# A sparse graph transformer on one core: turned x kept in weight places, five key stores, another GpSimd order

## The chip, the cores and the metric

The kernel runs on one core of one Trainium2 chip. The metric is the device time of one execution in microseconds (us), as the median of several runs; lower is better. The engines are named as in the profile: PE multiplies matrices, DVE is VectorE, ACT is ScalarE, POOL is GpSimd, SP is SyncE, which here only issues transfers.

## The reference

Two layers of a graph transformer on 2708 tokens of width 512, with 8 heads of 64 and a feed-forward width of 2048, all in float32. A token attends to its neighbours only: `adj` is a symmetric 2708 x 2708 int32 matrix with ones on the diagonal, in which an entry elsewhere is 1 with a chance of about 0.3%. So a token has some nine entries in its list, and 24 places are enough for the longest list.

```python
def layer(h, adj, ...):                       # twice, with weights of its own
    mask = adj.astype(jnp.float32) + jnp.eye(n)
    q = (h @ Wq.T + bq).reshape(n, 8, 64)     # k and v in the same way
    scores = jnp.einsum('nhd,mhd->hnm', q, k) / 8.0
    scores = jnp.where(mask[None] == 0, -1e9, scores)
    attn = jax.nn.softmax(scores, axis=-1)
    ctx = jnp.einsum('hnm,mhd->nhd', attn, v).reshape(n, 512)
    h1 = layer_norm(h + ctx @ Wo.T + bo, ln1_g, ln1_b)
    ff = relu(h1 @ W1.T + b1) @ W2.T + b2
    return layer_norm(h1 + ff, ln2_g, ln2_b)
```

## The kernel before, in words

**Tiles.** The tokens are cut into 22 tiles (`NT`) of up to 128; the last has 20 tokens. The kernel never forms the full score matrix. For each token it makes a list of neighbours, gathers their key and value rows from DRAM by indirect DMA, and multiplies on DVE and ACT. PE does the dense projections and the feed-forward.

**The first stage, `first`.** It works through the tiles in the order 20, 21, 0 to 19. For each it projects K and V on PE (L576) from blocks of the transposed input (`xg`, 256 tokens each, 11 blocks, 0.5 MB for a full one), adds the bias on the way into a tile `kvs` (K on DVE at L914, V on ACT), and stores `kvs` to the DRAM table `kv_d` through ACT's queue. Beside this run the lists (`lists`): SP loads 128 rows of the adjacency matrix (`aj`, 1.354 MB, two buffers), POOL adds the diagonal (L689), ACT squares it into codes (L693), and DVE finds the neighbours with MAX8 (L696). W1 and W2, the feed-forward weights, come in eight pairs of pieces, in places of their own in the pool `wts`: `w1_0` to `w1_7` and `w2_0` to `w2_7`, of 0.5 MB each. Until the weights arrive, some of these places hold other things. Before the change three of them (`w1_5` to `w1_7`) take the x blocks in rotation, three (`w2_5` to `w2_7`) the `kvs` tiles, and four (`w1_3`, `w1_4`, `w2_3`, `w2_4`) the tables of the lists.

**The second stage, `first_queries`.** It projects Q for every tile (tile 18 first, then 19, 20, 21, and 0 to 17; the counter is `j`, 0 to 21). As the three places of x have been turned over by then, nearly all x blocks are loaded a second time, by the same function `load`. DVE scales the result into `qs` (L977), which SP stores. Meanwhile the tokens are sorted by the length of their lists, so that tiles of similar tokens need few slots. DVE works out each token's new place (`ranks`, L803), POOL moves the lists of 21 tiles to their new places in the DRAM table `rec_d` by indirect DMA (L809), reads the table back as `new` (L823 and L831), and casts the token numbers to integers (`ident_i`, L842); from `new` DVE makes the row numbers `idx` and the mask `minus` (L845, L846, function `listed`). The first part of `listed` covers tiles 17, 18 and 19, the second the others.

**Attention ahead.** While PE projects Q, the function `advance` lets the generator `attend` run ahead. Tile 20 of the sorted order is made of the tokens of tile 18 as they stand, so it needs no sorting. `loads` issues the gathers (L1065, two slots of 128 rows of K and V to a chunk) and keeps `EARLY` = 3 chunks in flight ahead of the one in use; tile 20 has 18 slots, so 9 chunks (0 to 8). For each chunk, `weights` multiplies by q and sums by head on DVE (L1101, L1107), `weigh` takes the exponential and scales the values on ACT (L1120, L1127) and adds on DVE (L1133, L1140). After the last chunk come `sums` (L1148 to L1163) and `divided`, which writes the tile's result `cx` on ACT (L1171).

**The first feed-forward block.** The sorted tiles are worked on in pairs, `blocks`: (20, 19), (18, 17), (7, 9) and so on. For a pair `attended` turns `cx` on PE (L1241), multiplies by Wo (L576, output `o`), adds the gathered rows of x (`xb`, L1368), and norms (`va` on DVE at L1229, the power on POOL as `rd` at L1231, `h` on DVE at L1235). Then `feed_forward` goes through 16 slices `f`: first product (`pf`, L1433), relu on ACT (`ft`, L1444), second product (`a`, L1406). The attention of the next pair runs beside it, and its `cx` is wanted by PE at f=11 in the first block.

**What sets the order.** PE, ACT and SP run in the order of the program. POOL and DVE are ordered by a scheduler except inside `manual_schedule`, where they too keep the order of the program. DVE is pinned at the end of `first` and in `first_queries`, POOL through both and again in the blocks of layer 0. Every engine is in order when it runs: an instruction that waits holds up those behind it.

**POOL's order in the second stage**, which the change touches: 8 gathers of tile 20; 10 moves; then by turns 2 gathers, 2 moves, 2, 4, 2, 2, 2, 2; the last 2 gathers (chunk 8); the last move; the three reads of `new`; the cast; the gather of the own rows of tile 19 (`xr`); and the 5 gathers of tile 19.

Of the kernel before, what the change touches and what calls it, by code (L numbers as in the profile page):

```python
# [18 lines left out]
P = 128  # L19
# [453 lines left out]
def by_edges(ctx: ExitStack, tc: tile.TileContext, x, xT, adj, layers, out, good):  # L473
# [34 lines left out]
    at = None  # L508
# [95 lines left out]
    def lists_of(pa):  # L604


        room = {}

        def carve(where, words, *shape):
            if where not in room:  # L610
                t = wts.tile([P, NC, XB], F32, tag=where, name="lists")
                room[where] = [t.rearrange("p c n -> p (c n)"), 0]
            t, a = room[where]
            room[where][1] = a + words
            assert a + words <= NC * XB
            t = t[:, a : a + words]
            return t.rearrange("p (a b) -> p a b", b=shape[0]) if shape else t
# [14 lines left out]
        diag = carve("w2_3", P).bitcast(I32)  # L632
        nc.gpsimd.tensor_copy(diag, ident)
        parts = [(m, min(SEG, N - m)) for m in range(0, N, SEG)]
        eighth = carve("w2_3", NT * len(parts), len(parts))
        nc.gpsimd.memset(eighth[:, NT - 1, :], 0.0)
        top = carve("w2_3", NT * LIST, LIST)
        nc.gpsimd.memset(top[:, NT - 1, :], 0.0)
        rec = carve("w1_3", NT * 32, 32)
# [8 lines left out]
        by = carve("w1_3", LIST)  # L648
# [7 lines left out]
        tri = carve("w1_4", P)  # L656
# [54 lines left out]
        def counted():  # L711

            while full:
                kept()
            has = carve("w1_4", NT * LIST, LIST)
            nc.vector.tensor_scalar(has, top, 0.5, None, ALU.is_gt)
            low = top.bitcast(U16).rearrange("p t (e two) -> p t e two", two=2)[:, :, :, 0]
            count = carve("w1_3", NT)
            nc.vector.tensor_reduce(count, has, AX.X, ALU.add)
            nc.vector.tensor_tensor(rec[:, :, :LIST], has, low, ALU.mult)  # L720
            hot = carve("w2_4", NT * LIST, LIST)
            nc.vector.tensor_tensor(
                hot,
                count.unsqueeze(2).to_broadcast([P, NT, LIST]),
                by.unsqueeze(1).to_broadcast([P, NT, LIST]),
                ALU.is_equal,
            )
            nc.vector.memset(hot[:, STAR, :], 0.0)
            yield
            nc.gpsimd.tensor_copy(ident_i[:, FRESH : FRESH + 1], rec[:, STAR, LIST : LIST + 1])  # L730
            listed_as(slice(FRESH, FRESH + 1), rec[:, STAR : STAR + 1, :LIST])
            most = carve("w1_3", 1)
            before = has
            half = NT // 2
            halved = lambda big: big.rearrange("p (h t) e -> p h t e", h=2)
            b2, h2 = halved(before), halved(hot)
            nc.vector.memset(b2[:, :, 0, :], 0.0)
            for t in range(1, half):
                nc.vector.tensor_tensor(
                    b2[:, :, t, :], b2[:, :, t - 1, :], h2[:, :, t - 1, :], ALU.add  # L740
                )
            a2 = carve("w1_3", 2 * LIST, LIST)
            nc.vector.tensor_tensor(a2, b2[:, :, half - 1, :], h2[:, :, half - 1, :], ALU.add)
            nc.vector.tensor_tensor(
                b2[:, 1, :, :],
                b2[:, 1, :, :],
                a2[:, 0, :].unsqueeze(1).to_broadcast([P, half, LIST]),
                ALU.add,
            )
            a = carve("w1_3", LIST)  # L750
            nc.vector.tensor_tensor(a, a2[:, 0, :], a2[:, 1, :], ALU.add)
            run = carve("w1_4", LIST)
            nc.vector.memset(run[:, 0:1], 0.0)
            nc.vector.tensor_copy(run[:, 1:], a[:, : LIST - 1])
            step = 1
            while step < LIST:
                nxt = carve("w1_4", LIST)
                nc.vector.tensor_copy(nxt[:, :step], run[:, :step])
                nc.vector.tensor_tensor(
                    nxt[:, step:], run[:, step:], run[:, : LIST - step], ALU.add  # L760
                )
                run, step = nxt, 2 * step
            nc.vector.tensor_tensor(
                before, before, run.unsqueeze(1).to_broadcast([P, NT, LIST]), ALU.add
            )
            nc.vector.tensor_reduce(most, eighth, AX.XY, ALU.max)
            nc.vector.tensor_scalar(flags[:, 0:1], most, 0.5, None, ALU.is_le)
            yield hot, before, half

        def ranked(hot, before, half):  # L770

            places = carve("w1_3", NT)
# [25 lines left out]
            over = carve("w1_3", NT)  # L798
# [3 lines left out]
            ranks = carve("w1_3", NT).bitcast(I32)  # L802
# [56 lines left out]
    def first(w, meanwhile):  # L859
# [4 lines left out]
        stream += stream[:-1]  # L864

        def load():
            i = len(xg)
            b = stream[i] * XB
            bw = min(XB, N - b)
            t = wts.tile([P, NC, XB], F32, tag=f"w1_{5 + i % 3}", name="xg")  # L870
            xg.append(t)
            step = bw if i else P
            for a in range(0, bw, step):
                e = min(a + step, bw)
                nc.sync.dma_start(out=t[:, :, a:e], in_=chunked(xT)[:, :, b + a : b + e])
                yield

        def tokens(t, again):

            b, c0 = t * P // XB, t * P % XB  # L880
            i = stream.index(b) + (XBS if again and b != stream[XBS - 1] else 0)
            if c0 == 0 and i != XBS - 1 + again * XBS and len(xg) < len(stream):
                finish(load())
            xs = xg[i]
            return lambda c: xs[:, c, c0 : c0 + size(t)]
# [14 lines left out]
        lists, counted, ranked, listed = lists_of(pa.__enter__())  # L900
# [3 lines left out]
        for i, t in enumerate([NT - 2, NT - 1] + list(range(NT - 2))):  # L904
# [4 lines left out]
            xs = tokens(t, 0)  # L909
            kv = wts.tile([P, 2 * DM], F32, tag=f"w2_{5 + i % 3}", name="kvs")  # L910
# [11 lines left out]
            if i == 0:  # L922
                finish(load())
# [13 lines left out]
        at = ctx.enter_context(tc.tile_pool(name="at", bufs=2))  # L937
        return bq, wq, counts, ranked, listed, tokens

    def first_queries(bq, wq, counts, ranked, listed, tokens, meanwhile):  # L940

        made = []
# [18 lines left out]
        for j, t in enumerate(tiles):  # L961
            r = size(t)
            q = project(tokens(t, 1), r, wq, "q", other=j % 2 > 0)
# [17 lines left out]
            if j == 2:  # L981
                moving = ranked(*counts)
                for _ in range(8):
                    next(moving, None)
            if j > 2:
                advance(0.75)
                if j < 10:
                    next(moving, None)
                    next(moving, None)
                else:  # L990
                    finish(moving)
            if j == 11:
                xr = own_rows(order[1])
            if j == 18:
                listed(True)
                all_listed.append(True)
                advance(1.5)
            if j == 19:
                listed(False)
            if j == 20:  # L1000
                zT = turned_own(order[1], xr)
                own_query(order[1], zT, new_q(order[1]), bq, wq)
# [87 lines left out]
    class Tile:  # L1090
# [75 lines left out]
        def divided(self):  # L1166
            r = self.r
            cx = at.tile([P, DM], F32, tag="cx", name="cx", bufs=CXB)
# [8 lines left out]
    written = [[] for _ in range(NL)]  # L1177

    def rows_of_keys(n):
# [8 lines left out]
        if tag is None:  # L1188
            return at.tile([P, SLOTS, 2 * DM], F32, tag="kv", name="kv", bufs=KVB)
# [3 lines left out]
    def loads(n):  # L1193
# [3 lines left out]
        for g, s0, c in (chunk for g in order for chunk in chunks_of(g)):  # L1197
            r = size(g)
            if n == 0 and g == order[1] and s0 == 0:
# [16 lines left out]
            if len(ready) > EARLY:  # L1216
# [33 lines left out]
    class Layer:  # L1250
# [56 lines left out]
        def preloaded(self, tiles, temp):  # L1307
# [5 lines left out]
            places += [at.tile([P, DM], F32, tag="cx", name="zTs", bufs=CXB) for _ in range(CXB)]  # L1313
# [72 lines left out]
        def feed_forward(self, block, hs, hT):  # L1386
# [5 lines left out]
            if apart:  # L1392
                wide = [
                    at.tile([P, SLOTS, 2 * DM], F32, tag="kv", name="fts", bufs=KVB)
                    for _ in range(2)
                ]
# [76 lines left out]
        def keys_values(self, block, zs):  # L1473

            n = self.n + 1
            kvs = at.tile([P, SLOTS, 2 * DM], F32, tag="kv", name="kvs", bufs=KVB)
# [121 lines left out]
    def beside_keys(t):  # L1598
# [3 lines left out]
        if t > NT - 3:  # L1602
            now.load_second(t + 2 - NT, temp, sums)
            now.load_w1(t + 2 - NT)
            now.load_w2(t + 2 - NT)

    def beside_queries(j):
# [4 lines left out]
        if len(now.w2) < 3 or (j > 18 and len(now.w2) < 5):  # L1612
            now.load_w1(len(now.w1), nc.scalar)
            now.load_w2(len(now.w2), nc.scalar)
# [16 lines left out]
    with tc.manual_schedule(engines={mybir.EngineType.Pool}):  # L1631
        made = first(layers[0], beside_keys)
        with tc.manual_schedule(engines={mybir.EngineType.DVE}):
            first_queries(*made, beside_queries)
            early[0] = list(early[0])
    behind, pool = None, []
    for n in range(NL):
# [28 lines left out]
        in_order = ExitStack()  # L1666
        if n == 0:
            in_order.enter_context(tc.manual_schedule(engines={mybir.EngineType.Pool}))
        for k, block in enumerate(blocks):
# [4 lines left out]
            for f, zs in enumerate(now.feed_forward(block, hs, hT)):  # L1674
                if f == NFC:
                    break
                if f in (5, 6, 7, 8) and behind:
# [128 lines left out]
```

## Time and profile before

| What | Value |
|---|---|
| median of 3 runs | 1966.05 us (1965.59 to 1967.46) |
| the profiled execution | 1959.46 us, of which the span is 1957.3 us |
| instructions | 21027 |
| PE busy | 1849.3 us, 94% of the span |
| DVE busy | 1364.0 us, 70% |
| ACT busy | 959.0 us, 49% |
| POOL busy | 833.2 us, 43% |
| moved by DMA | 377.65 MB, 193 GB/s in the mean |
| loads of an adjacency tile | 21 of 1354.0 KB, 7.4 us to landing (median) |
| loads of a full x block | 19 of 512.0 KB, 6.5 us to landing |
| gathers of keys and values | 442, 1285 ns each on POOL, 5.8 us to landing |
| moves of lists | 21, 4.9 us to landing |

A line of the timeline has the start, the time taken, the engine, the line of the code, the operation, output and inputs by name, and in brackets the idle time ahead of it on that engine with what ended it. Times in a window's table are busy microseconds of each engine, with the number of instructions; the last three columns are the granted PE clock, the share of time in which the DMA engines were busy, and what they moved. [...]

### The profile page before, as it was taken

What the parts mean: (1) busy time and instruction counts of PE and PEld (TensorE: products, weight loads), DVE (VectorE), ACT (ScalarE), POOL (GpSimd) and SP (SyncE); (2) the same over time, 40 slices, a digit from 0 to 9 for tenths busy, and PEclk for the clock granted to TensorE, in tenths of its full rate; (3) what the DMA queues carried; (4) which work ended last, traced back from release to release, by engine and by line L of the source; (5) the groups of instructions that cost most, each with busy time, mean ns of one, the idle gap of its engine ahead of it and who ended that gap; (6) DMA issues with size and microseconds to landing.
All of it is one profiled execution on the core that took longest, in us unless ns stands there. A gap on an engine that the chain in (4) does not pass through costs nothing. (4 is left out here: it accounts for less than half of the span.)

```text
span 1957.3 us, 21027 instructions
## 1 busy us (share of the span) xinstructions
PE 1849.3 (94%) x6126; PEld 1093.7 (56%) x6126; DVE 1364.0 (70%) x2215; ACT 959.0 (49%) x3334; POOL 833.2 (43%) x732
## 2 busy tenths in 40 slices
PE   8899847999999999999999997999999999999997
PEld 3344315556566565665665553566566666666664
DVE  7887665759678796685750337686977999899522
ACT  4551325454546555474451113555475776666511
POOL 3114643536445455463410114444565665557101
PEclk9999978999999999999999999999999999999999
DMA  9998676656555665554411468555664776565000
GB/s 332 351 318 317 210 263 202 234 172 194 173 178 176 224 207 183 183 185 159 134 38 65 135 233 330 197 205 190 209 227 158 250 247 216 189 215 181 18 1 19
DMA packets 134031, 377.65 MB, mean 193 GB/s; under 512 B 17500, under 2 KB 36796, under 8 KB 131198
## 3 DMA queue, kind: packets, MB, share of 16 engines
q0 software_dynamic: 72176, 257.59, 39.3%
q1 hardware_dynamic: 52820, 99.14, 14.6%
q10 hardware_dynamic: 8910, 19.48, 2.7%
q8 instruction: 50, 0.82, 0.2%
q14 instruction: 75, 0.61, 0.1%
HBM read 325.35 MB, written 50.81 MB: 192 GB/s over the span
## 5 line engine op out<-in xcount | busy, mean ns | idle before, releaser
L1065 POOL DMA_INDIRECT kv<-kv_d,idx x442 | 567.9, 1285 | 477.4 <-DVE acc L1140 248.4
L1433 PE MATMUL pf<-hT,w 128*128 128x256 f32 (+1 forms) x2816 | 638.1, 374 | 11.4 <-ACT ft L1444 9.3
L1433 PEld LDWEIGHTS pf<-hT,w 128*128 128x128 f32 x2816 | 522.3, 192 | 185.6 <-issue 102.9
L1406 PE MATMUL a<-w,ft 128*128 128x512 f32 x1312 | 615.1, 595 | 6.6 <-ACT ft L1444 4.8
L1101 DVE TENSOR_TENSOR kv<-kv,q 128x1024 f32<-128x1024 f32 (+1 forms) x232 | 268.1, 1165 | 218.8 <-DMA kv<-kv_d,idx 182.6
L1406 PEld LDWEIGHTS a<-w,ft 128*128 128x128 f32 x1312 | 247.9, 191 | 197.7 <-issue 165.9
L1444 ACT ACTIVATE ft<-pf,b 128x256 f32<-128x256 f32 (+1 forms) x336 | 153.6, 463 | 417.2 <-PE pf L1433 416.9
L1127 ACT ACTIVATE kv<-kv,p 128x64 f32<-128x64 f32 x1328 | 335.3, 335 | 5.4
L1107 DVE TENSOR_REDUCE sc<-kv 128x16 f32<-128x1024 f32 (+1 forms) x232 | 267.5, 1161 | 2.0
L1140 DVE TENSOR_TENSOR acc<-acc,kv 128x1024 f32<-128x1024 f32 (+2 forms) x188 | 217.2, 1155 | 18.8 <-ACT kv L1127 16.0
L1231 POOL TENSOR_TENSOR rd<-va,mhalf 128x1 f32<-128x1 f32 (+1 forms) x88 | 94.1, 1069 | 283.1 <-DVE va L1229 282.1
L576 PE MATMUL o<-wo,cT 128*128 128x512 f32 x336 | 153.2, 609 | 20.8 <-ACT cT L1246 20.8
L1120 ACT ACTIVATE p<-sc,minus 128x8 f32<-128x8 f32 (+1 forms) x442 | 108.0, 293 | 113.5 <-DVE sc L1107 113.5
L1133 DVE TENSOR_TENSOR kv<-kv,p 128x512 f32<-128x512 f32 (+1 forms) x188 | 127.9, 681 | 20.7 <-ACT p L1120 20.7
L1171 ACT ACTIVATE cx<-acc,su 128x64 f32<-128x64 f32 (+1 forms) x352 | 88.6, 334 | 79.4 <-DVE su L1163 58.5
L576 PEld LDWEIGHTS o<-wo,cT 128*128 128x128 f32 x336 | 65.1, 196 | 104.1 <-issue 72.2
L693 ACT ACTIVATE code<-aj 128x2708 bf16<-128x2708 int32 (+1 forms) x22 | 71.0, 3228 | 47.5 <-POOL aj L689 41.6
L696 DVE MAX8 tops<-code 128x8 f32<-128x247 f32 (+2 forms) x242 | 83.8, 399 | 11.8 <-ACT code L693 11.7
L1235 DVE SCALAR_TENSOR_TENSOR h<-h,rd,ln_b 128x512 f32<-128x512 f32 (+1 forms) x88 | 65.6, 746 | 37.7 <-POOL rd L1231 37.7
L576 PE MATMUL k<-wk,xg 128*128 128x512 f32 x168 | 80.2, 623 | 11.1 <-DVE kvs L914 6.1
L1028 POOL DMA_INDIRECT kv_d<-kvs,ident_i x22 | 23.2, 1056 | 157.6 <-ACT kvs L1493 92.0
L1127 ACT ACTIVATE acc<-kv,p 128x64 f32<-128x64 f32 (+1 forms) x352 | 88.9, 334 | 1.4
(165 smaller groups left out, 1501.4 us busy)
## 6 DMA issues: line engine op xcount, KB each, us to landing
aj<-in_adj SPq DMA_DIRECT2D x21, 1354.0 KB, 7.4
kv_d<-kvs ACTq DMA_DIRECT2D x21, 512.0 KB, 6.2
w<-in_W SPq DMA_DIRECT2D x20, 512.0 KB, 7.7
xg<-in_xT SPq DMA_DIRECT2D x19, 512.0 KB, 6.5
kv<-kv_d,idx POOLq DMA_INDIRECT x442, 5.8
w<-in_W ACTq DMA_DIRECT2D x12, 512.0 KB, 6.8
q_d<-qs SPq DMA_DIRECT2D x23, 256.0 KB, 4.5
zT_d<-zT SPq DMA_DIRECT2D x22, 256.0 KB, 4.6
```

Of the source, the lines that this page charges most:

```text
L576: nc.tensor.matmul(o[:r], xs(c), wm[:, c, :], start=(c == 0), stop=(c == NC - 1))
L1065: return nc.gpsimd.indirect_dma_start(out=to, out_offset=None, in_=table[:, :], in_offset=bass.IndirectOffsetOnAxis(ap=s, axis=0), bounds_ ...
L1101: nc.vector.tensor_tensor(kv[:r, :c, :DM], kv[:r, :c, :DM], self.q[:r].unsqueeze(1).to_broadcast([r, c, DM]), ALU.mult,)
L1107: nc.vector.tensor_reduce(self.sc[:r, s0 : s0 + c, :], kv[:r, :c, :DM].rearrange("p s (h d) -> p s h d", d=DK), AX.X, ALU.add,)
L1120: nc.scalar.activation(p[:r, s, :], self.sc[:r, s, :], AF.Exp, bias=minus[:r, g, s : s + 1])
L1127: nc.scalar.activation(to[:, i, hd], kv[:r, i, DM + h * DK : DM + (h + 1) * DK], AF.Copy, scale=p[:r, s0 + i, h : h + 1],)
L1133: nc.vector.tensor_tensor(to[:, 0, :].rearrange("p (h d) -> p h d", d=DK), kv[:r, 0, DM:].rearrange("p (h d) -> p h d", d=DK), p[:r, s0, : ...
L1140: nc.vector.tensor_tensor(self.acc[:r, :c, :], self.acc[:r, :c, :], kv[:r, :c, DM:], ALU.add)
L1231: nc.gpsimd.tensor_tensor(rd[:r], va[:r], mhalf[:r], ALU.pow)
L1406: nc.tensor.matmul(a[:r], fts[f][:, c0 : c0 + r], self.w2[f // 2][:, f % 2, :], start=(f == 0), stop=(f == NFC - 1),)
L1433: nc.tensor.matmul(pf[:, :w], self.w1[f // 2][:, c, f % 2 * P : f % 2 * P + P], hT[:, c, :w], start=(c == 0), stop=(c == NC - 1),)
L1444: nc.scalar.activation(ft[:, :w], pf[:, :w], AF.Relu, bias=self.b1[:, f : f + 1])
```

## The change

1. *x blocks.* Each of the 11 blocks has a place of its own (`w2_0`, `w1_1`, `w2_1`, `w1_2`, ... `w1_5`, `w1_0`, in the order in which they are loaded) and stays there until its Q has been made. The second loading is gone: SP issues 12 x loads instead of 22 (the first block comes in two). One more block is loaded ahead of the first adjacency rows.
2. *W1 and W2 of layer 0.* Before, the first two pairs were loaded by SP at the end of `first`, the third by ACT's queue at j=0 and two more at j=19 and 20. After, ACT's queue loads five pairs between j=4 and j=20, as x blocks leave their places. The other three come in the first feed-forward block, as before.
3. *Keys.* `kvs` has five places in turn instead of three.
4. *Tables of the lists.* They lie in a pool of their own at the right end of memory, closed at j=9. The pool `above` takes the space: the three buffers `cx`, and one of the five buffers for gathered keys. So only four of these can be used until then.
5. *GpSimd order.* For tile 20 `loads` keeps two chunks in flight instead of three. POOL's order becomes: 6 gathers, 10 moves, then by turns 2 gathers, 2 moves, 2, 4, 2, 2, 2, 2, 2 gathers, the last move, the three reads of `new`, the cast, the 2 gathers of chunk 8, then `xr` and tile 19. The number of moves and gathers is the same.
6. *Steps of the second stage.* The two parts of `listed` come at j=17 and 18 instead of 18 and 19, and the own query of tile 19 at j=19 instead of 20.
7. *Pinned order.* POOL keeps the order of the program from `first` through layer 0 without a break, and DVE until f=5 of the first feed-forward block instead of until its start. In the order that results, the chunk weights of tiles 18 and 17 (five chunks), which stood on DVE among the operations of the first norms, come behind both norms; on POOL the gathers of `q` for these tiles come behind the two `rd`.

The core of the diff:

```diff
 def first(w, meanwhile):
         stream = [XBS - 1] + list(range(XBS - 1))
-        stream += stream[:-1]
+        homes = [f"w{1 + i % 2}_{i // 2}" for i in range(XBS)]
+        homes = homes[1:] + homes[:1]
...
-            t = wts.tile([P, NC, XB], F32, tag=f"w1_{5 + i % 3}", name="xg")
+            t = wts.tile([P, NC, XB], F32, tag=homes[i], name="xg")
...
-            i = stream.index(b) + (XBS if again and b != stream[XBS - 1] else 0)
-            if c0 == 0 and i != XBS - 1 + again * XBS and len(xg) < len(stream):
+            if c0 == 0 and len(xg) < XBS:
                 finish(load())
...
-            kv = wts.tile([P, 2 * DM], F32, tag=f"w2_{5 + i % 3}", name="kvs")
+            home = ("w2_5", "w2_6", "w2_7", "w1_6", "w1_7")[i % 5]
+            kv = wts.tile([P, 2 * DM], F32, tag=home, name="kvs")
...
             if i == 0:
                 finish(load())
+                finish(load())
             while done < min(NT, 1 + LEAD * i):
                 lists(done)
...
-        at = ctx.enter_context(tc.tile_pool(name="at", bufs=2))
+        at = ctx.enter_context(tc.tile_pool(name="at", bufs=2, reuse_waits="tile"))
 def first_queries(...):
-                if j < 10:
-                    next(moving, None)
-                    next(moving, None)
-                else:
+                if j < 9:
+                    for _ in range(2):
+                        next(moving, None)
+                elif above is None:
                     finish(moving)
+                    tables.__exit__(None, None, None)
+                    above = ctx.enter_context(
+                        tc.tile_pool(name="above", bufs=1, side="right", reuse_waits="tile")
+                    )
...
-            if j == 18:
+            if j == 17:
                 listed(True)
                 all_listed.append(True)
                 advance(1.5)
+            if j == 18:
+                listed(False)
             if j == 19:
-                listed(False)
-            if j == 20:
                 zT = turned_own(order[1], xr)
                 own_query(order[1], zT, new_q(order[1]), bq, wq)
 def room_of_keys(name):
+        if above is not None and len(rooms) < KVB:
+            rooms.append(f"kv{KVB - 1}")
+        tag = rooms.pop(0)
+        rooms.append(tag)
+        pool = above if tag == f"kv{KVB - 1}" else at
+        return pool.tile([P, SLOTS, 2 * DM], F32, tag=tag, name=name, bufs=1)
 def loads(n):
+            early = EARLY
+            if n == 0 and g == order[0]:
+                early = EARLY - 1
...
-            if len(ready) > EARLY:
+            if len(ready) > early:
                 yield ready.pop(0)
 def beside_keys(t):
         if t > NT - 3:
             now.load_second(t + 2 - NT, temp, sums)
-            now.load_w1(t + 2 - NT)
-            now.load_w2(t + 2 - NT)
 def beside_queries(j):
-        if len(now.w2) < 3 or (j > 18 and len(now.w2) < 5):
+        if j > 3 and len(now.w1) < (j - 2) // 4 + 1 < 6:
             now.load_w1(len(now.w1), nc.scalar)
+        if j > 3 and len(now.w2) < j // 4 and len(now.w2) < 5:
             now.load_w2(len(now.w2), nc.scalar)
...
-    with tc.manual_schedule(engines={mybir.EngineType.Pool}):
-        made = first(layers[0], beside_keys)
-        with tc.manual_schedule(engines={mybir.EngineType.DVE}):
-            first_queries(*made, beside_queries)
-            early[0] = list(early[0])
+    in_order, by_turns = ExitStack(), ExitStack()
+    in_order.enter_context(tc.manual_schedule(engines={mybir.EngineType.Pool}))
+    made = first(layers[0], beside_keys)
+    by_turns.enter_context(tc.manual_schedule(engines={mybir.EngineType.DVE}))
+    first_queries(*made, beside_queries)
+    early[0] = list(early[0])
...
-        in_order = ExitStack()
-        if n == 0:
-            in_order.enter_context(tc.manual_schedule(engines={mybir.EngineType.Pool}))
...
             for f, zs in enumerate(now.feed_forward(block, hs, hT)):
                 if f == NFC:
                     break
+                if f == 5:
+                    by_turns.close()
```

## The prediction

> **What bounds the kernel now.** I read the slices of the page first, then busy time by stage, then what PE waits for, then the timelines around the longest waits. Times are those of the profiled execution.
>
> ```profile
> PE   8899847999999999999999997999999999999997
> PEclk9999978999999999999999999999999999999999
> ```
> A digit is 49 us. PE is the bound nearly everywhere; the one deep hole, the sixth digit (245 to 294 us), is where the change is made.
>
> ```profile
> core 0: us, PE busy (x) PEld busy (x) DVE busy (x) ACT busy (x) POOL busy (x), PEclk, DMA share, GB/s
> 150.00:200.00 50.00, 50.00 (x127) 22.40 (x126) 34.23 (x72) 11.80 (x43) 24.42 (x20) 1.00 0.84 298
> 250.00:300.00 50.00, 17.78 (x44) 8.61 (x43) 31.43 (x43) 11.75 (x45) 19.17 (x20) 0.68 0.60 223
> 450.00:1000.00 550.00, 542.84 (x1823) 332.17 (x1822) 402.67 (x562) 298.83 (x1119) 272.43 (x216) 1.00 0.54 179
> ```
> PE idles 32 us in 250 to 300 and 7 us in 550 us of the steady part. So what moves the start of the first feed-forward block, FF-0, moves the end by as much; a microsecond saved on DVE or DMA elsewhere moves nothing.
>
> ```profile
> 274.05 5.87 PE L576 MATMUL o<-wo,cT 128*128 128x512 f32 x8 [19.90 <-ACT cT L1246]
> 289.15 1.12 PE L1241 MATMUL tp<-ident,h 128*128 128x128 f32 x4 [4.63 <-DVE h L1235]
> 297.03 1.12 PE L1241 MATMUL tp<-ident,h 128*128 128x128 f32 x4 [6.77 <-DVE h L1235]
> 298.61 9.00 PE L1433 MATMUL pf<-hT,w 128*128 128x256 f32 x32 [0.46 <-ACT hT L1246]
> 342.74 3.78 PE L1433 MATMUL pf<-hT,w 128*128 128x256 f32 x8 [9.30 <-ACT ft L1444]
> ```
> The brackets give the idle time ahead and its releaser: 20 us for the attention of tile 19, 5 and 7 for the two norms, then 9.3 us at f=11 for tiles 18 and 17. Backwards from there:
>
> ```profile
> 228.47 1.46 POOL L809 DMA_INDIRECT rec_d<-lists  x1 [0.30 <-issue]
> 234.56 0.86 POOL L823 DMA_DIRECT2D new<-rec_d  x1 [4.63 <-DMA rec_d<-lists]
> 245.89 1.01 POOL L1065 DMA_INDIRECT kv<-kv_d,idx  x1 [6.32 <-ACT cx L1171]
> ```
> ```profile
> 234.21 1.23 DVE L1101 TENSOR_TENSOR kv<-kv,q 128x1024 f32<-128x1024 f32 x1 [3.17 <-DMA kv<-kv_d,idx]
> 244.91 0.22 DVE L845 TENSOR_SCALAR idx<-new 128x72 int32<-128x72 f32 x1
> 257.04 1.23 DVE L1101 TENSOR_TENSOR kv<-kv,q 128x1024 f32<-128x1024 f32 x1 [6.03 <-DMA kv<-kv_d,idx]
> 271.49 0.20 DVE L1163 RECIPROCAL su<-su 128x8 f32<-128x8 f32 x1
> ```
> POOL is the first limit: ranks are known at 177.7, its 21 moves and 10 gathers run 180.40 to 229.93, then comes the read-back. DVE runs tile 20's last chunk (chunk 8) from 234.21, then `idx` at 244.91; POOL gathers tile 19 from 245.89, and DVE starts on it at 257.04. The gathers named "ACT cx" wait for `idx` in fact.
>
> **What the Trainium skill says.** "DMA: Bandwidth & Descriptors", section "Issuing engines are not separate DMA queues": transfers started by any engine end on the same 16 DMA engines. The trace agrees: DMA share is 0.90, 0.96 and 0.96 in the three 50 us stretches before 150, whoever issues. So moving W1 and W2 from SP to ACT saves no transfer. "GPSIMD Engine Reference", section "Specifications": GpSimd shares its SBUF interfaces with VectorE and contends with DVE instructions that have two SBUF inputs. The trace fits: the six indirect DMAs issued in 199 to 207, with DVE idle until 206.68, take 1.01 to 1.04 us; beside products and sums they take up to 2.08. "TensorE: Matmul & The Clock Gate", section "Part 1: The HAM clock gate (the "warmup" mystery)": an idle window of about 3.4 us lowers the clock. Here 20 us of idleness are followed by 5.87 us for an `o` that next takes 3.70; as long a hole costs the same after the change.
>
> **The change part by part.**
>
> 1. *x stays on chip.* In the listing of both kernels' instructions SP's x loads go from 22 to 12, 5.0 MB less. No PE wait on them is among the large waits of 0 to 420 us, so the removal itself is worth 0. One more 0.5 MB block now goes out ahead of the first adjacency rows, on SP's queue. These stretches are at 0.90 to 0.96 of DMA, so every adjacency tile lands later by about 0.512 MB / 0.358 MB per us (358 GB/s moved in 50 to 100) = 1.4 us. PE's 6.1 us stall at 59 to 65 us (a key eviction behind the MAX8 of list 7 on DVE) grows by that; bounds 0 and 1.4, I take **+1.4** for the end of K/V and the ranks (179.1).
> 2. *W1/W2.* The four loads at 144 to 150 on SP and the later ones on ACT become ten on ACT between j=4 and j=20. ACT waits there for PE to have read an x block of an earlier j; what stands behind on ACT is tile 20's weighing, whose `q` evictions come later on DVE anyway. FF-0 needs none before 298. 5.2 MB take the place of 5.0 MB of x: **0**; bounds -1 and +1.
> 3. *Five places for keys.* The instructions of K/V keep their order on PE, DVE and ACT, and the one stall there isn't for a place: **0**, bounds -1 and 0. Tables on the right side: same instructions, **0**. Before j=9 tile 20 has four key buffers instead of five, with one chunk less in flight: **0**, covered by POOL, which sets the pace.
> 4. *POOL's order.* Six instead of eight gathers come ahead of the moves: 2 x 1.30 us off, but the moves then wait for the ranks: start 179.3 instead of 180.40 (-1.1). The same 31 instructions at the same 49.5 us end at 228.8; 4.6 us to landing, 2.7 us of read-back, `ident_i` at 236.2. Only now come the two gathers of chunk 8 that stood at 225.06 to 228.17: 236.5 to 239.1, landed at about +5.1 us. DVE starts chunk 8 at **244.2** instead of 234.21: +10.
> 5. *What follows from it.* DVE needs 10.5 us from there to `idx` as before, which still stands behind chunk 8 although `listed` is called earlier: 254.7. Gathers of tile 19 from 255.5 (+9.6). Their landing took 11.15 us at 245.89, beside the W loads issued at 243 to 247, which are gone; I take 9.0, between the page's median of 5.8 and that (both ends: 261.3 to 266.7), so weights start at 264.5 (+7.5). The evictions of j=19 and 20 and the own query (now one tile earlier) stand there too: PE's waits on `qs` grow by 5 to 10 us, but PE has nothing on the path until tile 19. The 1.6 us wait for `bo` at 270.46 ends inside the delay, and the reciprocal comes at 277 (**+5.3**).
> 6. *DVE and POOL pinned into FF-0.* In before, five chunk weights of tiles 18 and 17 (1.2 + 1.2 us each) stood among the operations that lead to `h`: the scheduler had put them at 272.96 to 286.9. All five now come behind both norms, and the `q` gathers behind both `rd`. On the way from `o` to the first `rd` (287.28) they cost three times 1.2 us between `h<-o,xb` and `va`, and about 0.8 us ahead of it: **-4.4** (bounds -3.6 and -5), first `rd` at 287.28 + 5.3 - 4.4 = 288.2. The second `xb` is still issued behind the first `rd` and lands 4 us later, so FF-0 starts at 299.5: **+0.9**.
> 7. *Inside FF-0.* Those 12.2 us now fall into it. DVE's idle time there was 7.9 us before 304.89, then 2.7 and 5.9. `q` of tile 18 lands about 3 us after the start, so 2.9 us fit ahead of what came at 304.89, and 9.3 go into 8.6: **+0.7** at f=11.
>
> Sum: 0.9 + 0.7 = **+1.6**. After 400 us PE is the bound and carries it. The profiled execution took 1959.46 us (span 1957.3), 6.6 below the median of the three runs; I put the sum on the median: 1966.05 + 1.6 = **1967.6**. A measurement of this kernel can tell about 0.2%, 3.9 us, from no change.
>
> **The rivals.**
>
> *A, forecast: +1.6, own range 1961 to 1974* (the bounds above, and 4 us either way for landings that the trace of before cannot show).
>
> *B, slower: FF-0 cannot hide the five weights.* ACT is in order: the exponentials of tile 18 stand among the `ft`, and wait for the moved weights. For it: DVE becomes a closed chain there, and the stall at f=11 exists already. Against: DVE idled 21 of 50 us in 300 to 350. If the 9.3 us add whole, 0.9 + 9.3 = +10.2, **1976**. It decides from the point where tile 17's reciprocal (340.08, 41.5 us after the start) comes later than 46 us after it.
>
> *C, faster: POOL runs free.* All 31 at the 1.3 us pitch of the quiet ones take 40.3 instead of 49.5 us; 9.2 us earlier through the chain gives 1.6 - 9.2 = -7.6, **1958**. For it: one chunk less on DVE in that stretch. Against: the other seven chunks still run beside. Shorter landings of tile 19 would add 3 us.
>
> *D: the change saves no traffic on the path*, as W takes x's place: that is within A.
>
> **How the numbers follow.** A 0.46 (within 0.2% 0.22, slower 0.15, faster 0.09), B 0.27, C 0.27: faster 0.36, same 0.22, slower 0.42. Cases of both signs hold most of the chance; the likeliest one's own range stands above. For 8 in 10 the range takes in B and C with 4 to 5 us beyond: **1953 to 1980**.
>
> **What would show it.** Right: 12 x loads on SP; the stall at 59 to 65 us grown to some 7.5; moves from about 179, `ident_i` near 236, chunk 8's weights near 244, tile 19's first gather near 255, first `rd` near 288, FF-0 near 299.5, a stall at f=11 near 10. Wrong: chunk 8 before 238 (then C), a stall at f=11 above 15 (then B), a K/V stage that ends before 163, or PE below 98% busy between 450 and 1000 us.

## The result, and the profile after

The kernel after took **1980.87 us** in the median of 7 runs (1973.53 to 1985.50), the kernel before 1965.97 us on the same chip (1958.18 to 1967.46). The ratio is 1.0079 (95% interval 1.0058 to 1.0100): **15 us slower**. The forecast was 1967.6, with 1980 as the upper end. The profiled execution took 1979.62 us with a span of 1977.7, which is 20 us above the profiled execution of before. That one lay 6.6 us below its median, so some 5 us of what the two traces differ by are no loss.

The slices and the stages of after:

```profile
PE   9799758899999999999999997999999999999997
PEclk9899979899999999999999999999999999999998
```
```profile
core 0: us, PE busy (x) PEld busy (x) DVE busy (x) ACT busy (x) POOL busy (x), PEclk, DMA share, GB/s
150.00:200.00 50.00, 50.00 (x127) 22.36 (x126) 30.75 (x70) 9.29 (x33) 21.29 (x19) 1.00 0.55 193
250.00:300.00 50.00, 25.98 (x57) 11.56 (x57) 26.58 (x48) 13.36 (x52) 17.79 (x19) 0.70 0.55 199
...
450.00:1000.00 550.00, 534.94 (x1785) 326.51 (x1784) 396.17 (x553) 291.34 (x1084) 263.81 (x214) 0.99 0.54 177
```
The hole at 250 to 300 is no deeper. The last row is the surprise: PE now idles 15 us in 550 us of the steady part, where it idled 7. The slices of the page hide it, because each still reads 9.

Now the chain that the prediction followed, on PE, POOL and DVE of after:

```profile
279.88 6.11 PE L576 MATMUL o<-wo,cT 128*128 128x512 f32 x8 [11.06 <-ACT cT L1260]
298.40 1.11 PE L1255 MATMUL tp<-ident,h 128*128 128x128 f32 x4 [7.22 <-DVE h L1249]
299.97 9.76 PE L1446 MATMUL pf<-hT,w 128*128 128x256 f32 x32 [0.46 <-ACT hT L1260]
...
327.21 1.99 PE L1446 MATMUL pf<-hT,w 128*128 128x256 f32 x8 [1.98 <-ACT ft L1457]
341.09 1.99 PE L1446 MATMUL pf<-hT,w 128*128 128x256 f32 x8 [2.93 <-ACT ft L1457]
```
```profile
225.53 1.92 POOL L800 DMA_INDIRECT rec_d<-rec,ranks  x1 [0.31 <-issue]
232.89 0.86 POOL L814 DMA_DIRECT2D new<-rec_d  x1 [5.44 <-DMA rec_d<-rec,ranks]
...
254.28 0.99 POOL L1065 DMA_INDIRECT kv<-kv_d,idx  x1 [14.47 <-issue]
```
```profile
243.23 1.23 DVE L1101 TENSOR_TENSOR kv<-kv,q 128x1024 f32<-128x1024 f32 x1 [6.73 <-DMA kv<-kv_d,idx]
...
253.32 0.22 DVE L836 TENSOR_SCALAR idx<-new 128x72 int32<-128x72 f32 x1
...
265.59 1.22 DVE L1101 TENSOR_TENSOR kv<-kv,q 128x1024 f32<-128x1024 f32 x1
...
277.26 0.20 DVE L1163 RECIPROCAL su<-su 128x8 f32<-128x8 f32 x1
```
Chunk 8 starts at 243.23 (forecast 244.2), the gathers of tile 19 at 254.28 (255.5), the reciprocal stands at 277.26 (277) and the first feed-forward block at 299.97 (299.5). Up to here the prediction holds to about a microsecond in its numbers, though two of its steps went otherwise (see the part on why it was wrong). The time is lost later. Read the start of the operation that ends a norm (`h<-h,rd,ln_b`, the ones of full tiles counted through the kernel) in each trace:

| norm no. | before, us | after, us | after less before |
|---|---|---|---|
| 1 (first block's) | 288.3 | 289.7 | +1.4 |
| 11 | 527.4 | 528.5 | +1.1 |
| 19 | 694.9 | 701.6 | +6.7 |
| 27 | 849.0 | 858.6 | +9.6 |
| 40 (near the end of layer 0) | 1098.2 | 1114.6 | +16.4 |
| 84 (last) | 1946.4 | 1966.5 | +20.1 |

All but 1.4 us of the loss in layer 0 falls behind 530 us, in a part of the program where the diff changes no computation. One place (norm 19 of the table and the one behind it), first in before, on PE, DVE and POOL, then in after:

```profile
679.57 7.03 PE L576 MATMUL o<-wo,cT 128*128 128x512 f32 x16
```
```profile
686.61 0.68 DVE L1368 TENSOR_TENSOR h<-o,xb 128x512 f32<-128x512 f32 x1
```
```profile
694.24 0.59 POOL L1231 TENSOR_TENSOR rd<-va,mhalf 128x1 f32<-128x1 f32 x1
```
```profile
701.13 0.66 PE L1241 MATMUL tp<-ident,h 128*128 128x128 f32 x4 [0.32 <-DVE h L1235]
```

And after:

```profile
682.43 7.03 PE L576 MATMUL o<-wo,cT 128*128 128x512 f32 x16
```
```profile
692.75 0.68 DVE L1384 TENSOR_TENSOR h<-o,xb 128x512 f32<-128x512 f32 x1
```
```profile
689.11 1.75 POOL L1065 DMA_INDIRECT q<-q_d,ident_i  x1 [2.27 <-DVE kv L1101]
691.16 0.99 POOL L1065 DMA_INDIRECT kv<-kv_d,idx  x1 [0.30 <-issue]
...
697.10 1.93 POOL L1065 DMA_INDIRECT kv<-kv_d,idx  x1 [0.30 <-DVE mv L1241]
699.33 1.62 POOL L1065 DMA_INDIRECT kv<-kv_d,idx  x1 [0.30 <-issue]
700.98 0.60 POOL L1245 TENSOR_TENSOR rd<-va,mhalf 128x1 f32<-128x1 f32 x1
```
```profile
708.40 1.12 PE L1255 MATMUL tp<-ident,h 128*128 128x128 f32 x4 [4.74 <-DVE h L1249]
```
At its `o` PE is already 2.9 us late (679.57 in before, 682.43 in after). DVE turns to this norm at 686.61 and 692.75, 3.3 us more than that, since work on the chunks of the next tiles stands ahead of it. The power `rd` then waits 2.8 us for POOL in after (its input `va` is ready at 698.2), in before 2.1: a `q` gather and six key gathers in a row are ahead of it, and the `q` gather, which waits for DVE to be done with an older `q`, starts 6.7 us later than in before (682.43). The second norm takes 0.5 us more. So PE, which had waited 0.3 us for it, waits 4.7. The order of the two programs says why this can differ: in the two traces, counted behind the second norm, some 240 of DVE's 1622 operations stand in another place, and 22 of POOL's 600. The diff shows none of this; a scheduler made it. It could do so on POOL too, for POOL's pinned order ends with the first feed-forward block and not with layer 0 as stated ahead: in both kernels `in_order.close()` stands inside the loop over the blocks.

The waits are not the whole loss either. Of the 20.4 us between the two spans 11.7 are idle time of PE; the other 8.7 are its busy time, 1858.0 us instead of 1849.3 for the same 6126 instructions. In part this is the granted clock (the column PEclk):

```profile
core 0: us, PE busy (x) PEld busy (x) DVE busy (x) ACT busy (x) POOL busy (x), PEclk, DMA share, GB/s
708.00:711.40 3.40, 3.00 (x7) 1.93 (x8) 3.40 (x5) 2.01 (x8) 1.26 (x1) 0.50 0.68 212
871.90:875.30 3.40, 3.40 (x5) 1.34 (x5) 3.40 (x4) 3.40 (x15) 1.99 (x2) 0.50 0.56 182
1032.30:1035.70 3.40, 3.40 (x6) 1.34 (x5) 0.68 (x1) 1.78 (x7) 0.00 (x0) 0.50 0.00 0
```
These three stretches at half the clock begin within 1 us of the ends of three waits of PE, of 4.74, 2.28 and 1.96 us (at 708.40, 871.18 and 1031.72), where before waits 0.32, 0.83 and 0 us; both traces have one more such stretch between 450 and 1100 us, near 675. In the second of the three, eight matmuls of `a` take 5.40 us, where four had taken 1.88 at 867.01. If PE does half the work there, the three cost some 5 us (an estimate, 3 times half of 3.4).

### The profile page after: what moved, and what is told of

It reads as the page before. It is cut to its first block, busy times and chain, and to the rows that moved or that the text cites. A ratio compares the mean times of both kernels' runs of the same rounds, so it can differ in the third digit from the quotient of the medians.

```text
span 1977.7 us, 20995 instructions
## 1 busy us (share of the span) xinstructions
PE 1858.0 (94%) x6126; PEld 1094.8 (55%) x6126; DVE 1363.1 (69%) x2215; ACT 960.4 (49%) x3334; POOL 829.6 (42%) x732
## 5 line engine op out<-in xcount | busy, mean ns | idle before, releaser
L1419 PE MATMUL a<-w,ft 128*128 128x512 f32 x1312 | 622.6, 600 | 12.5 <-ACT ft L1457 10.1
L684 ACT ACTIVATE code<-aj 128x2708 bf16<-128x2708 int32 (+1 forms) x22 | 71.0, 3227 | 50.3 <-POOL aj L680 48.5
L576 PE MATMUL k<-wk,xg 128*128 128x512 f32 x168 | 79.6, 618 | 15.2 <-DVE kvs L908 10.6
```

The source lines that it names most:

```text
L576: nc.tensor.matmul(o[:r], xs(c), wm[:, c, :], start=(c == 0), stop=(c == NC - 1))
L1419: nc.tensor.matmul(a[:r], fts[f][:, c0 : c0 + r], self.w2[f // 2][:, f % 2, :], start=(f == 0), stop=(f == NFC - 1),)
```

## The experiments

Theory S said that the steady loss comes from the five buffers for gathered keys. Before, they have one name, and a tile gets whichever is free. After, they have five names that `room_of_keys` hands out in fixed turn, because one of them lies in another pool. Theory M said that the memory plan for x, W1/W2 and the tables does it. All ratios are against the kernel before, run on the same chip in the same measurement; a microsecond figure beside a ratio is that ratio's excess times 1964.

**e1_rooms**: five names in fixed turn, and nothing else.

```diff
+    rooms = [f"kv{i}" for i in range(KVB)]
...
+        tag = rooms.pop(0)
+        rooms.append(tag)
+        return at.tile([P, SLOTS, 2 * DM], F32, tag=tag, name=name, bufs=1)
...
-            return at.tile([P, SLOTS, 2 * DM], F32, tag="kv", name="kv", bufs=KVB)
+            return room_of_keys("kv")
...
```


> The kernel before, with one edit: the five buffers for gathered keys have five names, taken in fixed turn, instead of one name with five buffers of which any free one is given out. Nothing of x, W1/W2, the key stores, the tables or the pinning is changed. The DVE and POOL order of the rest of layer 0 (behind the first block) then differs from before in 146 of 251 differing rows of after. Theory S (the scheduler's new order or the fixed turn of the buffers in the steady part of layer 0 is what costs the 15 us): slower than before by 5 to 15 us, first feed-forward block unmoved (within 1 us of 298.6), loss between 500 and 1150 us. Theory M (the memory plan: x kept, W1/W2 late on ACT, tables, four key buffers): within 2 us of before.

Measured: 1974.75 us against 1964.14, ratio **1.0054** (1.0036 to 1.0073), +10.6 us. Norm 1 comes 1.0 us late, norm 40 13.2 us. This one edit, which moves no byte and adds no operation, makes most of the loss, in the same place as in after.

**e2_order**: before with the edits that give it after's order on DVE and POOL behind the first norms, and none of the memory plan for x.

That is the edit of e1_rooms, the pinning of e3_pin below, the loop of the moves as in after, and the earlier steps:

```diff
-            if j == 18:
+            if j == 17:
                 listed(True)
...
-            if j == 20:
+            if j == 19:
                 zT = turned_own(order[1], xr)
```


> The kernel before with the pinned order (DVE to f=5, POOL without a break), `listed` and own query one tile earlier, the moves' loop, and the five named key buffers, but x loaded twice, W1/W2 as before, three key stores, tables in weight places, three chunks in flight for tile 20. Behind the first norms its DVE and POOL orders are those of after, instruction by instruction. Theory S: the loss in layer 0 between 500 and 1150 us is that of after, about 14 us, and as chunk 8 keeps its early place and the norms are freed of the chunk weights, the first feed-forward block starts 4 us earlier: in all +8 to +12 us. Theory M: only the earlier start shows, -4 to 0 us.

Measured: ratio 1.0012 (1.0003 to 1.0022), +2.4 us. Norm 1 comes 9.2 us early and norm 40 3.2 us late: 12.4 us are lost between them, as in e1_rooms, and without anything of the memory plan but the named buffers. The front gained more than I had expected, so the sum fell short of the +8 to +12; the loss behind it is that of theory S.

**e3_pin**: before, pinned.

```diff
...
+                if f == 5:
+                    by_turns.close()
...
```


> The kernel before with one edit: DVE pinned to f=5 of the first block and POOL without a break. Tests step 6 of the prediction by itself. The prediction's working: first rd 4.4 us earlier, FF-0 starts 3 to 4.5 us earlier, 0.7 us given back inside: -2 to -4 us if the steady part keeps its pace. The DVE order behind the first norms differs from before in 83 rows (after: 251). Theory S: part of that is lost again, a third of 14 us: -4 + 5 = about +1. Theory M: -3.

Measured: ratio **0.9960** (0.9945 to 0.9976), 1957.4 us, 6.7 us faster in the medians. From `o` to the first `rd` it takes 8.6 us instead of 13.2: step 6 of the prediction had taken out 4.4, and 4.6 went. Norm 40 is 3.6 us early, so in this trace the 83 rows of DVE's order that differ cost next to nothing. (What the edit does on POOL is to join its pinned stretches; behind the first block the scheduler orders it, as before.)

**e4_x_as_before**: after, with x loaded twice, W1/W2 as before, three key stores and one x block less ahead of the first adjacency rows.

```diff
-            t = wts.tile([P, NC, XB], F32, tag=homes[i], name="xg")
+            t = wts.tile([P, NC, XB], F32, tag=f"w1_{5 + i % 3}", name="xg")
...
+            now.load_w1(t + 2 - NT)
+            now.load_w2(t + 2 - NT)
...
```


> The kernel after, with its memory plan for x undone: x blocks in three places and loaded twice, W1/W2 loaded as before, three key stores, one block less ahead of the first adjacency rows. Tables on the right side, four key buffers until j=9, POOL order, named buffers and pinning stay. DVE and POOL orders behind the first norms are those of after. Theory S: as slow as after, +13 to +16 us against before (1.4 us less for the block loaded ahead). Theory M: within 3 us of before.

Measured: ratio 1.0037 (1.0023 to 1.0051), +7.3 us. Its trace loses 14.0 us between norms 1 and 40, like after. With e2_order, which loses as much without the plan, theory M is out for the steady part. But the ratio is some 8 us better than after's, with intervals apart, which neither theory gave. What of x costs is asked again below, and these 8 us stay without a shown cause.

**e5_turn**: as e1_rooms, five names of one buffer each, but the turn written out as before had it. A letter is a buffer, in brackets when it takes the next layer's keys (`kvs` of `keys_values`), read from the addresses in the built programs:

```
before, e5   A B C E D (A) B C A E D B C A E D (B) C A B E D
e1           A B C D E (A) B C D E A B C D E A (B) C D E A B
```
The next layer's keys need a buffer only for a short time. Before fills it again three gathers later; the fixed turn leaves it idle until its place comes, five gathers later, so the gathers between have one buffer less to run ahead with.

> The kernel of e1_rooms (five named key buffers, everything else as before), with the turn of the five names copied from the buffers that the kernel before got from its one name: after a tile of the next layer's keys, its buffer is used again three gathers later and is not left idle until its turn. The DVE and POOL orders then stand within 21 and 4 rows of before (e1_rooms: 146 and 19). Theory T (the fixed turn, with the order that the scheduler made for it, costs the time): the loss of 10 us of e1_rooms goes, within 3 us of before. Theory N (names of one buffer each cost by themselves, whatever the turn): still +8 to +12 us.

Measured: ratio **1.0008** (0.9996 to 1.0020). The loss is gone: 2.4 us between norms 1 and 40 instead of 12.2. At the place shown above, POOL and PE of this kernel read:

```profile
695.92 0.59 POOL L1240 TENSOR_TENSOR rd<-va,mhalf 128x1 f32<-128x1 f32 x1
```
```profile
702.81 0.66 PE L1250 MATMUL tp<-ident,h 128*128 128x128 f32 x4 [1.43 <-DVE h L1244]
```
Between 450 and 1100 us its clock has the stretch near 675 and none of the three others. So it isn't the names but the turn, with the order that the scheduler makes for it.

**e6_after_turn**: after, with the turn of before from the first tile of the next layer's keys on.

```diff
-    rooms = [f"kv{i}" for i in range(KVB - 1)]
+    rooms = iter(
...
-        tag = rooms.pop(0)
-        rooms.append(tag)
+        tag = f"kv{next(rooms)}"
...
```
The string in `iter` is the turn of before, with the names changed.

> The kernel after with one edit: from the first tile of the next layer's keys on, the five key buffers are used in the turn of the kernel before (renamed), not in a fixed turn. All other parts of the change stay. Theory T: the loss of some 14 us between 500 and 1100 us goes; what is left is the front, +1.4 us at the first feed-forward block: 0 to +4 us against before. Rival (the pinning, the late start or the memory plan cost in the steady part): still +10 us or more.

Measured: ratio **1.0017** (1.0006 to 1.0028), +3.3 us, where after has 1.0079. Its trace has none of the three half-clock stretches either. So the fixed turn costs the kernel after 0.62%, 12 of its 15 us.

**e7_pin_listed**: e3_pin, with `listed` and the own query one projection earlier.

> The kernel before with two parts of the change: the pinned order of DVE and POOL into the first block (as e3_pin), and `listed` and the own query of tile 19 one projection earlier. Key buffers, x, W1/W2, POOL's gathers and moves as before. From the front of e2_order (first rd 9.2 us earlier) and the steady part of e3_pin: -9 to -12 us against before, and 2 to 5 faster than e3_pin. Rival: a later wait takes the front's gain back (as the 9.3 us stall at f=11 would): -5 us, as e3_pin.

Measured: ratio **0.9951** (0.9932 to 0.9970), 1952.43 us against 1962.13. It beats both kernels by these two parts of the change alone. In its trace PE's `o` starts 26.6 us after `idx`, in e3_pin 29.1, so the earlier steps bring 2.6 us at the front; the ratios of the two don't part them.

**e8_one_less**: after, with two x blocks ahead of the first adjacency rows.

```diff
             if i == 0:
                 finish(load())
-                finish(load())
```


> The kernel after with one edit: the second extra x block isn't loaded ahead of the first adjacency rows (two blocks ahead, as before, not three). The K/V stall at 59 to 69 us shrinks from 10.6 to 6.3 us, as in e4_x_as_before. Theory: the first feed-forward block starts 2 us earlier, and the end comes 2 to 4 us before that of after, so +11 to +13 us against before. Rival: nothing is left of it by the first block, since POOL sets the pace from 170 us on: as after, +15 us.

Measured: ratio 1.0082 (1.0061 to 1.0103), no better than after. The stall went from 10.6 to 6.2 us and norm 1 came 1.5 us earlier, but at the end nothing can be told.

**e9_mended, e10_two_chunks, e11_three_chunks**: three steps between e7_pin_listed and after. e9 is after with before's turn, three chunks in flight and two blocks ahead; e11 has the third block again; e10 is before with two chunks in flight, the reverse of this edit of e9 and e11:

```diff
...
-                early = EARLY - 1
+                early = EARLY
...
```


> The kernel after with three edits: the turn of the key buffers as in e6_after_turn, three chunks in flight for tile 20 as before (so that the gathers of chunk 8 stand ahead of the last move again), and two x blocks ahead of the first adjacency rows as before. It differs from e7_pin_listed in the memory plan alone: x kept on chip, W1/W2 on ACT from j=4, five key stores, tables on the right side, four key buffers until j=9; behind the first norms the orders of the two differ in 21 rows on DVE and 4 on POOL. Theory: the memory plan is worth nothing either way, so as e7_pin_listed, -8 to -10 us against before. Rival: the plan costs (W1/W2 on ACT's queue or four buffers hold up tile 20): -4 us or worse.

> The kernel before with one edit: two chunks in flight for tile 20, so that the two gathers of chunk 8 stand behind the read-back and the cast. Order behind the first norms as before. The prediction's steps 4 and 5 by themselves: chunk 8's weights 9 to 10 us later (near 244), first rd and the first feed-forward block 5 to 8 us later (the 4.4 us that the pinned order takes out are not there), and +5 to +8 us at the end. Rival: the 9.3 us stall at f=11 takes it up: 0 to +2 us.

> As e9_mended, but with the third x block ahead of the first adjacency rows, as in after. Against e9_mended it has the price of that block alone. From the K/V stalls (10.6 against 6.3 us) and the first norms (after 2 us behind e4_x_as_before): 2 to 4 us slower than e9_mended, thus -4 to -8 us against before. Against e6_after_turn it has the price of chunk 8's late gathers alone: 8 to 10 us faster than e6_after_turn.

Measured: e9 0.9974 (0.9963 to 0.9985), e11 0.9982 (0.9973 to 0.9990), e10 **1.0029** (1.0019 to 1.0039). DVE of e10:

```profile
241.28 1.23 DVE L1101 TENSOR_TENSOR kv<-kv,q 128x1024 f32<-128x1024 f32 x1 [6.54 <-DMA kv<-kv_d,idx]
...
251.97 0.22 DVE L845 TENSOR_SCALAR idx<-new 128x72 int32<-128x72 f32 x1
```
Chunk 8 starts 7 us later than in before, norm 1 comes 7.0 us later, and 5.7 us are left at the end: the stall at f=11 takes up little. Against e6_after_turn, e11 has the price of the same step in after, 0.35% or 6.9 us. The extra block is 0.08% (e11 against e9), with intervals that overlap.

**e12_mended_x**: e9_mended with x, W1/W2 and stores as before.

> The kernel of e9_mended with the x half of the memory plan undone: x in three places and loaded twice, W1/W2 loaded as before, three key stores. Tables on the right side, the pool above and four key buffers until j=9 stay. e9_mended came 4.5 us behind e7_pin_listed, with the loss in layer 1. Theory X (x, W1/W2 or the stores cost it): as e7_pin_listed, -8 to -10 us against before. Theory P (the tables, the pool above and the buffers cost it): as e9_mended, -4 to -6 us.

Measured: 0.9965 (0.9954 to 0.9976), between e7 and e9, with intervals that meet both. The memory plan as a whole comes to 0.23% (e9 against e7), 4.5 us, also with intervals that overlap; which half of it costs stays open. In the one trace of e9 it isn't in layer 0 at all (norm 40 is 8.7 us early, in e7 7.9) but in layer 1 (norm 84 is 2.1 early, in e7 7.7), in part as waits and in part as busy time of PE.

The plan and the extra block together, e11 against e7, are 0.31% or 6.1 us, and there the intervals just don't overlap (up to 0.9970, from 0.9973). So together they are not free; how the cost divides isn't shown.

From e7_pin_listed to after, one step at a time (each ratio is against before on its own chip, so the steps compare measurements on different chips):

| kernel | ratio | step | us |
|---|---|---|---|
| e7_pin_listed | 0.9951 | pinning, earlier steps | -9.6 |
| e9_mended | 0.9974 | memory plan | +4.5 (not told from 0) |
| e11_three_chunks | 0.9982 | one x block more ahead | +1.6 (not told from 0) |
| e6_after_turn | 1.0017 | chunk 8 behind the read-back | +6.9 |
| after | 1.0079 | fixed turn of the key buffers | +12.2 |

That these steps add up is by their making. What supports the two large ones is that each was also measured alone in before: +10.6 us (e1_rooms) and +5.7 (e10_two_chunks).

## Why the prediction was wrong

**The step that failed** is in part 3, "Before j=9 tile 20 has four key buffers instead of five, with one chunk less in flight: **0**", with the sentence that closes the sum: "After 400 us PE is the bound and carries it." I priced the new naming of the key buffers until j=9 only, and took the steady part as given since PE is busy 98.7% there. But the same naming hands the buffers out in fixed turn through both layers, and the orders of DVE and POOL behind the first norms change with it. That PE is busy says how little there is to win; it doesn't keep a new wait from being added, and behind new waits came stretches at half the clock. The term I set at 0 measures +10.6 us alone (e1_rooms) and +12.2 in after (against e6_after_turn). The listing of the two programs had shown the changed order without a run; I compared it for the front and not behind it. What the runs leave open is how the 12 us divide between waits for the buffers themselves and the order that the scheduler made for the turn: e5_turn changes both at once. The waits of `q` gathers on POOL, 9.0 us in before and 32.5 in after between 480 and 1080 us, aren't it by themselves, as e5_turn still has 22.4.

**The other steps.**

- *Part 1*, one block more ahead: the K/V stall grew by 4.4 us (6.1 to 10.6), not 1.4, so the ranks come 3.3 us later and the moves start at 181.23, not 179.3. That they end at 227.45, before the 228.8 of the forecast, is luck: the 31 instructions took 46.2 us in this execution, not 49.5. In e6_after_turn, with the same front, they took 48.5, and the first block starts at 301.60, 2.1 us behind the forecast. At the end the block's price can't be told from 0 (+1.6 us in e11 against e9, -0.6 in after against e8).
- *Parts 4 and 5*, chunk 8 behind the read-back: forecast +5.3 us at tile 19's reciprocal, measured 277.26 - 271.49 = +5.8; e10 alone ends 5.7 us later. The size is right. The working has slips: +7.5 less 1.6 is +5.9 and not 5.3, and from chunk 8 to `idx` before took 10.7 us, not 10.5. And the start of tile 19's weights came near its number by another wait than the one that was priced, the landing of its gathers (9.0 us). DVE gets to it at 265.59 straight from evicting the own query and another `q`, ahead of which it had stood idle for 5.55 and 2.74 us. In e8_one_less, which has the same order, two such waits (5.46 and 2.74 us, both for PE) stand ahead of the weights at 264.13, and there the first gather, issued at 252.91, had landed after 7.7 us. So the hit at the reciprocal is in part luck.
- *Part 5*, earlier `listed`: I counted only the 1.6 us of `bo`. From tile 19's first weights to `o` it takes 14.3 us in after and 17.0 in before, 2.7 in all.
- *Part 6*, the pinned order: right to 0.2 us (e3_pin).
- *Part 7*, +0.7 us in FF-0: wrong in sign. The stall of 9.3 us became two of 2.0 and 2.9, and the block ended 0.6 us nearer to before than it began (+0.8 at the fourth norm). In e3_pin the same block gains 2.5 us.
- *Rival B* had the right sign and, by its 1976, nearly the size, but not the mechanism: the five weights are hidden.

## What to carry to other kernels

When buffers with one name become buffers with names of their own, ask who else draws on them: a tile that holds a buffer briefly costs nothing where any free one is given out, and a place in every turn where the turn is fixed. Compare the order of every engine to the end of the program, not only where the diff stands, before calling a stage "bound by PE and unmoved"; at 98.7% busy there were 7 us to win, which says nothing of how much can be lost. And price the parts of a large change apart: here two of them alone were worth -10 us, and two others spent it twice over.

## What the runs showed of the hardware

One 0.5 MB transfer more ahead of the first adjacency rows lengthened the K/V stall by about 4 us: it is 4.4 to 7.1 us in before, e1 to e5, e7 to e10 and e12, and 9.8 to 10.6 in after, e6 and e11, which alone have that block. At the 358 GB/s moved in that stretch it would be 1.4. Why it is three times as much the runs don't say. A gather or move on POOL took 1.0 us at best and up to 2.0 in after too (the move at 191.63).
